# First attention of a two-layer kernel: the sums of a step's weights are taken behind the next step's scores

## The chip, the cores and the metric

The kernel runs on one core of one Trainium2 chip. A core has a matrix engine (TensorE, PE in the profile, with PEld for its loads of weights), a vector engine (VectorE, DVE), a scalar engine (ScalarE, ACT), GpSimd (POOL), and a sync engine (SyncE, SP) whose queue issues most of the transfers. Each engine works through its own queue in order, and engines wait for each other by semaphores. Matmuls write into PSUM, which this kernel cuts into two pairs of banks and four single banks; everything else lies in SBUF.

The metric is device time in microseconds. The kernel before takes 1857.02 us, the median of three runs (1854.37 to 1859.17).

## The reference

Two transformer layers follow each other on x of 4 sequences, 512 tokens, 512 channels, all in float32. Each adds an attention part and a feed-forward part to x. The change touches only the attention of the first layer:

```
def _L0_attn_ref(x, W_qkv, W_o):          # x is layer-normed before
    B, T, C = x.shape                      # 4, 512, 512
    H = 16
    D = C // H                             # 32
    qkv = jnp.einsum('btc,oc->bto', x, W_qkv).reshape(B, T, 3, H, D)
    ...
    q = _rms_norm(q * cos + _rotate_half(q) * sin)
    k = _rms_norm(k * cos + _rotate_half(k) * sin)
    scores = jnp.einsum('bhqd,bhkd->bhqk', q, k) * scale
    scores = jnp.where(causal[None, None], scores, jnp.float32(-1000000000.0))
    attn = jax.nn.softmax(scores, axis=-1)
    out = jnp.einsum('bhqk,bhkd->bhqd', attn, v)
    ...
    return jnp.einsum('btc,oc->bto', out, W_o)
```

Behind it come a gated feed-forward part with weights rounded to three values, a second layer whose attention part is a scan over time, and a second feed-forward part with an attention of its own and routed experts. They fill the span from about 424 us on.

## The kernel before

The four sequences (batches b = 0 to 3) go through the first attention one after another, from 65 to 408 us of the profile. `attend` (L345) works on one batch. Its 16 heads are taken in four groups g of four heads, and the 512 keys in four blocks j of 128. A step m is one pair (g, j), so a batch has 16 steps, and steps 4g to 4g+3 belong to group g. Because of the causal mask, key block j is met only by the queries from 128 j on: 512, 384, 256 or 128 of them.

Five small functions make up a step:

- `scores` (L355): PE multiplies queries and keys of four heads into two pairs of banks (L361). ACT takes the exponentials into the tile `pt` of that j (L366), which has one buffer. POOL then puts zeros where a query precedes its key (L367, the mask).
- `weigh` (L372): PE adds the values, weighted with `pt`, to the group's averages `av` (L377), which stay in one bank from the group's first step to its end.
- `add` (L382): for j > 0, DVE adds the weights of the block before to those of this block (L385), in place. After it, the first 128 queries of `pt` hold their sum over all key blocks, still spread over the 128 keys of a block.
- `invert` (L387): PE multiplies these 128 queries with ones, which sums over the keys (L392, into a bank `sm`), and DVE takes the reciprocals (L396). At the group's last step DVE multiplies the averages with the reciprocals into `oT` (L398), which frees the bank of `av`.

The loop from L401 to L411 lays the steps out with a lag. Within turn m of the loop:

```
scores(*steps[m])          # the new step
add(*steps[m - 2])
part()                     # what between[m] holds
weigh(*steps[m - 1])
invert(*steps[m - 2])
```

`between` (built from L458 on) holds the work of other batches that is put between the steps: projections of the next batch (`project`, eight matmuls of 128x512 at L284, 3.70 us in all, whose result DVE reads for the rotation at L296 and L300), the output projection of the batch before (`back`, L340 and L343), transposes of heads (`turn_heads`, through `transpose_into` at L132 and L133), the scaling of heads on DVE (`scale_heads`, L312 to L327), and jobs on the weights of the feed-forward part. Such a job fetches a piece of weights through SP (L218) and measures it on ACT (L234, L252) or rounds it on DVE (L201, L202); two pieces are under way at a time. Batch 3 has no projections to put in, and from its step 5 on no output projections either.

Inside this stage PE's order is that of the program text (`manual_schedule` at L417). The order on DVE, ACT and POOL is set by a planner, which simulates the kernel before it runs, keeps roughly to the program's order and pulls instructions ahead where its model has an engine free. The planner also chooses which of the four single banks a tile gets. These banks serve `av`, `sm`, the projections `pq` and `y`, and the transposes `tp`.

After the loop `attend` returns a function that ends the last step; the caller lays two transposes of heads of the next batch ahead of it (L483 to L486).

Of the kernel before, what the change touches and what calls it, by code (L numbers as in the profile page):

```python
# [46 lines left out]
def block_kernel(ctx: ExitStack, tc: tile.TileContext, a: dict, out: bass.AP):  # L47
# [16 lines left out]
    def pair(name):  # L64
        return banks["pair"].tile([P, 2, 512], F32, tag="pair", name=name)

    def bank(name):
        return banks["bank"].tile([P, 512], F32, tag="bank", name=name)
# [95 lines left out]
    with tc.tile_pool(name="a_w", bufs=1) as aw, tc.tile_pool(name="a_1", bufs=1) as a1, tc.tile_pool(  # L164
# [180 lines left out]
        def attend(b, between):  # L345

            qkT, v = turned_qk[b], values[b]
            oT = outs[b] = a1.tile([P, NK, T], F32, tag="oT", name="oT")
            weights, averages, inverses = {}, {}, {}

            def scores(g, j):  # L355
                w = T - j * P
                pt = weights[g, j] = a2.tile([P, HG, w], F32, tag=f"pt{j}", name=f"pt{j}", bufs=1)
                both = [pair("sc") for _ in range(2)]
                for i in range(HG):
                    rows = slice(i * D, (i + 1) * D)  # L360
                    nc.tensor.matmul(  # L361
                        both[i // 2][:, i % 2, :w], qkT[rows, NG + g, j * P : (j + 1) * P],
                        qkT[rows, g, j * P :], start=True, stop=True,
                    )
                for i, sc in enumerate(both):
                    nc.scalar.activation(pt[:, 2 * i : 2 * i + 2, :w], sc[:, :, :w], AF.Exp, scale=SCALE)  # L366
                nc.gpsimd.affine_select(  # L367
                    out=pt[:, :, 0:P], in_=pt[:, :, 0:P], compare_op=ALU.is_ge, fill=0.0,
                    base=0, pattern=[[0, HG], [1, P]], channel_multiplier=-1,
                )  # L370

            def weigh(g, j):  # L372
                if j == 0:
                    averages[g] = bank("av")
                for i in range(HG):
                    h = g * HG + i
                    nc.tensor.matmul(  # L377
                        averages[g][i * D : (i + 1) * D, j * P :], v[:, j, h * D : (h + 1) * D],
                        weights[g, j][:, i, :], start=j == 0, stop=j == NT - 1,
                    )  # L380

            def add(g, j):  # L382
                if j > 0:
                    pt = weights[g, j]
                    nc.vector.tensor_tensor(pt, pt, weights[g, j - 1][:, :, P:], ALU.add)  # L385

            def invert(g, j):  # L387
                if j == 0:
                    inverses[g] = a2.tile([P, T], F32, tag="r", name="r", bufs=1)
                sm = bank("sm")  # L390
                for i in range(HG):
                    nc.tensor.matmul(  # L392
                        sm[i * D : (i + 1) * D, :P], ones[:, :D], weights[g, j][:, i, :P],
                        start=True, stop=True,
                    )
                nc.vector.reciprocal(inverses[g][:, j * P : (j + 1) * P], sm[:, :P])  # L396
                if j == NT - 1:
                    nc.vector.tensor_tensor(oT[:, g, :], averages.pop(g), inverses.pop(g), ALU.mult)  # L398

            steps = [(g, j) for g in range(NG) for j in range(NT)]  # L400
            for m in range(len(steps) + 1):  # L401
                if m < len(steps):
                    scores(*steps[m])
                if m > 1:
                    add(*steps[m - 2])
                for part in between.get(m, ()):
                    part()
                if m > 0:
                    weigh(*steps[m - 1])
                if m > 1:  # L410
                    invert(*steps[m - 2])  # L411
            return lambda: (add(*steps[-1]), invert(*steps[-1]))

        def do(f, *args):
            return lambda: f(*args)
# [1 line left out]
        with tc.manual_schedule(engines={mybir.EngineType.PE}):  # L417
# [39 lines left out]
            for b in range(B):  # L457
# [20 lines left out]
                if b == B - 1:  # L478
                    first_mv = const.tile([P, NT, 2], F32, tag="mv", name="mv")
                    for t in range(NT):  # L480
                        between[9].append(do(statistics, a1, xs[0], t, first_mv))
                finish = attend(b, between)
                if b + 1 < B:  # L483
                    turn_heads(b + 1, 2)
# [302 lines left out]
    with tc.tile_pool(name="b_s", bufs=1) as bs, tc.tile_pool(name="b_1", bufs=1) as b1, tc.tile_pool(  # L787
# [79 lines left out]
        with tc.manual_schedule(engines={mybir.EngineType.PE}):  # L867
# [4 lines left out]
            for b in range(B):  # L872
# [10 lines left out]
                def part(n):  # L883
                    if n % 3 == 2 and n > 3 * 4 and b + 1 < B:
                        next(coming, None)
                        if not light[0]:
                            return
                    if n not in (2, 3, 5):
                        light[0] = next(between, False)
# [194 lines left out]
    with tc.tile_pool(name="c_1", bufs=1, reuse_waits="tile") as c1, tc.tile_pool(  # L1084
# [7 lines left out]
        steps = [(b, n, half) for b in range(B) for n in range(NS) for half in range(2)]  # L1092
# [730 lines left out]
```

## Time and profile before

| what | value |
|---|---|
| time, median of three runs | 1857.02 us |
| the profiled execution | 1858.7 us, with a span of 1857.0 us |
| mean granted TensorE clock | 0.98 |
| first attention | 65 to 408 us |
| sums, L392 on PE | 512 matmuls, median 273 ns, eight to a step |
| reciprocals, L396 on DVE | 64, median 950 ns |
| additions, L385 on DVE | 48, from 622 to 2205 ns, for 512, 1024 or 1536 elements |
| exponentials, L366 on ACT | 128, from 363 to 1026 ns, two to a step |
| mask, L367 on POOL | 64, median 635 ns, at most 2165 ns |
| product into oT, L398 on DVE | 16, median 691 ns |

A row of the timeline has the start in us, the length in us, the engine, the line, the operation, output and inputs with their shapes, and the number of instructions merged into it; in brackets stands how long the engine had been idle and what ended that. Neighbouring matmuls overlap a little at their ends, so from start to start they take somewhat less than their rows say. A row of the waits has the waiting engine, line and tile, what it waited for, and then the total in us, the number of times and the longest. A wait before a load of weights (PEld) is counted apart from PE's own.

### The profile page before, as it was taken

The numbers are of one execution on the slowest core, as the hardware profiler recorded it, in microseconds if no ns is written. First come the engines' busy times: TensorE is split into PE (matmuls) and PEld (weight loads), VectorE is DVE, ScalarE is ACT, GpSimd is POOL, SyncE is SP. The second block draws the span as 40 slices with busy tenths as digits, with TensorE's granted clock in tenths as the row PEclk, the third lists the DMA queues.
The fourth block names the chain that finished last, engine by engine and source line by source line (L and its number), as shares of the span: only waits on it lengthen the run. The fifth ranks groups of instructions, "written<-read, shape, count | busy, mean of one in ns | idle before, by whom it ended". The sixth has DMA issues, their size and how long they took to land.

```text
span 1857.0 us, 27575 instructions
## 1 busy us (share of the span) xinstructions
PE 1740.2 (94%) x10374; PEld 1093.0 (59%) x10374; DVE 1186.6 (64%) x1908; ACT 938.0 (51%) x1940; POOL 581.5 (31%) x383
## 2 busy tenths in 40 slices
PE   7899899989999998989997989999999999999998
PEld 3443344437777676878886875556556554544444
DVE  6577757786655556899887886574766764322222
ACT  2433533332242536889988867576676652111111
POOL 2231313120202021889887860100000000244431
PEclk9999999999999999999999988999999999999999
DMA  7002300102011112333223200000010006455545
GB/s 244 22 1 68 109 1 1 46 1 76 5 40 53 59 56 82 94 92 102 58 73 102 58 28 1 1 24 1 1 35 24 24 24 230 150 91 91 91 79 142
DMA packets 74630, 115.07 MB, mean 62 GB/s; under 512 B 9546, under 2 KB 34762, under 8 KB 73940
## 3 DMA queue, kind: packets, MB, share of 16 engines
q1 hardware_dynamic: 64996, 90.87, 15.4%
q0 software_dynamic: 8656, 20.32, 6.1%
q10 hardware_dynamic: 848, 2.13, 0.3%
q8 instruction: 83, 1.36, 0.3%
q14 instruction: 47, 0.39, 0.1%
HBM read 83.02 MB, written 33.42 MB: 63 GB/s over the span
## 4 chain that ended last, share of the span: by engine, by line
PE 68%; DVE 13%; ACT 11%; issue 3%; DMA 3%; POOL 1%; DVEq 0%; SPq 0%; ACTq 0%; POOLq 0%
PE pgr L1702 7%; PE pg L844 6%; PE pq L284 5%; PE ys L1153 4%; PE yr L1723 4%; PE scd L1387 4%; PE bu L1121 3%; PE y L1327 3%; PE y L862 3%; PE pge L1288 3%; PE tp L132 3%; PE bu L1116 3%; PE y L340 3%; PE tpd L1410 2%; ACT pr L1398 2%
## 5 line engine op out<-in xcount | busy, mean ns | idle before, releaser
L1140 POOL TENSOR_TENSOR hc<-h,cb 128x1024 f32<-128x1024 f32 x128 | 301.1, 2378 | 115.4 <-DVE h L1129 93.7
L1129 DVE TENSOR_TENSOR_SCAN h<-da,bu 128x512 f32<-128x512 f32 x256 | 295.1, 1204 | 28.5 <-PE bu L1121 14.3
L284 PE MATMUL pq<-wqkv,hT 128*128 128x512 f32 x384 | 179.6, 615 | 4.8 <-DVE qk L300 3.6
L1109 ACT ACTIVATE da<-delta_l,am 128x511 f32<-128x511 f32 x256 | 163.4, 709 | 2.1 <-DVE h L1129 2.0
L1398 ACT ACTIVATE pr<-scd,nm 128x128 f32<-128x128 f32 (+3 forms) x256 | 133.3, 530 | 57.6 <-DVE nm L1395 56.7
L844 PE MATMUL pg<-hTh,w 128*128 128x512 f32 (+1 forms) x352 | 145.6, 414 | 1.0 <-ACT hTh L831 0.7
L844 PE MATMUL pg<-hTl,w 128*128 128x512 f32 (+1 forms) x352 | 139.9, 397 | 0.2 <-DVE hTl L832 0.2
L1153 PE MATMUL ys<-ident,hc 128*128 128x128 f32 x1024 | 136.7, 277 | 3.3 <-DVE h L1129 1.7
L1121 PE MATMUL bu<-ident,bu 128*128 128x128 f32 x768 | 132.2, 279 | 6.4 <-ACT bu L1103 6.4
L1702 PE MATMUL pgr<-wgu,gTe 128*128 x304 | 137.1, 593 | 0.0
L1103 ACT ACTIVATE bu<-dxT,bts 128x512 f32<-128x512 f32 x192 | 124.3, 712 | 16.2 <-PE bu L1121 13.3
L284 PEld LDWEIGHTS pq<-wqkv,hT 128*128 128x128 f32 x384 | 71.5, 194 | 97.3 <-issue 91.2
L366 ACT ACTIVATE pt<-sc 128x1024 f32<-128x1024 f32 (+3 forms) x128 | 83.3, 698 | 78.0 <-PE sc L361 72.3
L1387 PE MATMUL scd<-kTd,qTd 32*128 32x512 f32 (+3 forms) x512 | 109.0, 507 | 14.0 <-ACT pr L1398 11.3
L1153 PEld LDWEIGHTS ys<-ident,hc 128*128 128x128 f32 x1024 | 119.0, 143 | 4.3 <-DVE h L1129 1.9
L1116 PE MATMUL bu<-diag_l,dxT 128*128 128x128 f32 x512 | 105.9, 289 | 16.3 <-DVE h L1129 13.3
L367 POOL TENSOR_SCALAR_AFFINE_SELECT pt<-pt 128x512 f32<-128x512 f32 x64 | 56.2, 879 | 179.1 <-ACT pt L366 156.5
L1395 DVE TENSOR_REDUCE nm<-scd 128x2 f32<-128x256 f32 (+3 forms) x128 | 105.0, 821 | 2.8
L1410 PE MATMUL tpd<-ident,pr 128*128 128x128 f32 x640 | 102.6, 290 | 3.5 <-ACT ptd L1417 1.1
L1116 PEld LDWEIGHTS bu<-diag_l,dxT 128*128 128x128 f32 x512 | 82.3, 196 | 40.0 <-DVE h L1129 23.2
L1121 PEld LDWEIGHTS bu<-ident,bu 128*128 128x128 f32 x768 | 95.6, 145 | 9.9 <-ACT bu L1103 9.9
L1709 DVE SCALAR_TENSOR_TENSOR hidr<-pgr,silr 128x256 f32<-128x256 f32 x38 | 16.1, 425 | 130.0 <-ACT silr L1707 130.0
(338 smaller groups left out, 3290.7 us busy)
## 6 DMA issues: line engine op xcount, KB each, us to landing
cb<-c_rows SPq DMA_DIRECT2D x64, 256.0 KB, 3.3
q_w<-in_w2T SPq DMA_DIRECT2D x20, 256.0 KB, 2.8
diag_l<-diags SPq DMA_DIRECT2D x64, 64.0 KB, 2.0
hrows<-h SPq DMA_DIRECT2D x4, 1024.0 KB, 4.3
acc<-x SPq DMA_DIRECT2D x16, 256.0 KB, 2.0
wgu<-in_r_gate SPq DMA_DIRECT2D x7, 512.0 KB, 9.5
wgu<-in_r_up SPq DMA_DIRECT2D x7, 512.0 KB, 10.0
wdn<-in_r_down SPq DMA_DIRECT2D x7, 512.0 KB, 9.3
```

The source lines that it names most:

```text
L284: nc.tensor.matmul(y, inputs_T[b][:, k, t * P : (t + 1) * P], wqkv[:, k, s * C : (s + 1) * C], start=k == 0, stop=k == NK - 1,)
L844: nc.tensor.matmul(pg[:rows, i, :], w[:, k, f * P : f * P + rows], part[:, k, :], start=k + m == 0, stop=k + m == NK,)
L1109: nc.scalar.activation(da[:, k, 1:], delta[:, k, 1:], AF.Exp, scale=am[:, k, n : n + 1])
L1116: nc.tensor.matmul(bu[:, :P], loaded[b][1][:, 0, k * P : (k + 1) * P], scaled[b, n][0], start=True, stop=True,)
L1121: nc.tensor.transpose(bu[:, t * P : (t + 1) * P], scaled[b, n][t][:, k * P : (k + 1) * P], ident)
L1129: nc.vector.tensor_tensor_scan(h[:, i, :], decays[b, n][:, 2 * half + i, :], bu, 0.0, ALU.mult, ALU.add)
L1140: nc.gpsimd.tensor_tensor(hc, states.pop((b, n, half)), weighed[b, n].unsqueeze(1).to_broadcast([P, 2, T]), ALU.mult)
L1153: nc.tensor.matmul(sums[b][t][:, k * P : (k + 1) * P], hc[:, i, t * P : (t + 1) * P], ident, is_transpose=True, start=n == 0 and k == 0, s ...
L1387: nc.tensor.matmul(sc[:, i, :w], qT[at, g, t * P : w], kT[at, g, :w], start=True, stop=True)
L1398: nc.scalar.activation(pr[:, i, :w], sc[:, i, :w], AF.Exp, bias=nm[:, i : i + 1], accum_out=sums[b, g][:, t, 2 * p + i : 2 * p + i + 1],)
L1410: nc.tensor.transpose(tp[:, j * P : (j + 1) * P], pr[:, i, j * P : (j + 1) * P], ident)
L1702: nc.tensor.matmul(pg, gT[:, k, :], wgu[:, bass.ds(e, 1), k, :].rearrange("p e o -> p (e o)"), start=k == 0, stop=k == NK - 1,)
```

## The change

In turn m of the loop the sums of step m - 3 are now taken right after the new step's scores and the addition, ahead of the other batches' work, where before those of step m - 2 ended the turn. Turn m = 16, which has no scores, takes the sums of step 13. After the loop the last addition and the sums of step 14 are laid down at once, and the function that is returned only takes the sums of step 15.

```diff
                     scores(*steps[m])
                 if m > 1:
                     add(*steps[m - 2])
+                if m > 2:
+                    invert(*steps[m - 3])
                 for part in between.get(m, ()):
                     part()
                 if m > 0:
                     weigh(*steps[m - 1])
-                if m > 1:
-                    invert(*steps[m - 2])
-            return lambda: (add(*steps[-1]), invert(*steps[-1]))
+            add(*steps[-1])
+            invert(*steps[-2])
+            return lambda: invert(*steps[-1])
```

On PE the order of two turns reads, before and after (w, s and p for the averages, the sums and the other batches' work):

```
before:  scores m | p | w m-1 | s m-2 | scores m+1 | p | w m | s m-1
after:   scores m | s m-3 | p | w m-1 | scores m+1 | s m-2 | p | w m
```

## The prediction

> **What bounds the kernel now.** The page's head comes first, for the whole span.
>
> ```profile
> span 1857.0 us, 27575 instructions
> PE 1740.2 (94%) x10374; PEld 1093.0 (59%) x10374; DVE 1186.6 (64%) x1908; ACT 938.0 (51%) x1940; POOL 581.5 (31%) x383
> PE 68%; DVE 13%; ACT 11%; issue 3%; DMA 3%; POOL 1%; DVEq 0%; SPq 0%; ACTq 0%; POOLq 0%
> ```
>
> The second line is busy time, the third the chain that ended last. TensorE (PE) bounds the kernel, so a change pays where PE stands still. The change touches only the first attention. Its windows, one for each batch, were cut at the batches' first scores; the columns are the stretch, its length, then PE, PEld, DVE, ACT and POOL busy, and the granted clock.
>
> ```profile
> 65.00:151.50 86.50, 80.04 (x531) 34.65 (x529) 63.80 (x104) 34.66 (x57) 25.00 (x25) 0.98 0.00 1
> 151.50:258.70 107.20, 97.11 (x565) 41.86 (x563) 79.92 (x131) 47.16 (x92) 25.82 (x25) 0.97 0.26 77
> 258.70:350.90 92.20, 89.37 (x548) 38.23 (x546) 59.96 (x96) 32.11 (x53) 24.15 (x24) 1.00 0.00 1
> 350.90:407.20 56.30, 47.31 (x425) 19.19 (x418) 45.59 (x55) 21.34 (x33) 14.49 (x16) 0.96 0.13 38
> ```
>
> PE idles 6.5, 10.1, 2.8 and 9.0 us in them, 28.4 us in all: nothing above that can come from this stage. What ended PE's idle time is in the waits, from 65 to 408 us:
>
> ```profile
> PE sm L392 <- DVE pt L385: 13.2, 15, 1.9
> PE sc L361 <- ACT pt L366: 4.2, 4, 1.8
> PE pq L284 <- DVE qk L300: 3.6, 1, 3.6
> PE av L377 <- POOL pt L367: 3.3, 2, 1.7
> ```
>
> The first row is what the change aims at: the sums (`invert`, L392) wait 15 times for VectorE's addition (`add`, L385). The likely gain is therefore a part of 13.2 us, and I go through the 15 places.
>
> **The change, part by part.** No instruction is added or removed and no DMA moves. In each batch the sums of steps 0 to 12 now stand behind the next step's scores instead of in front of them; those of 13, 14 and 15 keep their place on PE, since no scores follow there. So 52 of the 64 groups of sums trade places with one group of scores. On PE the cover that a wait gains is exactly those scores: 1.07, 0.86, 0.65 or 0.44 us from start to start for 512, 384, 256 or 128 queries (1.14, 0.93, 0.71 and 0.50 us in the rows, ends overlapping). A group of sums itself takes 0.35. On DVE the reciprocal (L396, 0.95 us) and every fourth step the product into `oT` (L398, 0.69) now come behind the next step's addition in program order. POOL and SP get nothing new. The last addition is issued ahead of two heads' transposes; the sums that need it there (148.16 us) wait for nothing now, so this is worth 0.
>
> *Ends of batches 0, 1 and 2.* Six of the 15 waits are the sums of steps 13 and 14, 0.90 and 0.62 us each time (144.17, 145.44; 251.21, 252.47; 346.61, 347.88): 4.6 us. Their order on PE is the same afterwards: gain 0.
>
> *Start of batch 0.* Before the sums of step 2 at 81.40 PE waits 0.90 us; then come scores and, at 83.01, a projection. In the new order scores 4 start at 77.85 (before 79.00), because two groups of sums come behind them and not ahead. Scores 5 then wait for the exponentials of step 4 (1.94 us for the two, L366, ending at 80.9) and end at 81.5; the sums follow, and the projection starts at 81.85. Gain 83.01 - 81.85 = 1.15 us. What follows to 150 us is PE-bound, with no DMA, so it is kept.
>
> *Steps 9 of batches 0 and 2* (109.35, 311.57; 0.55 us each). The scores cover the wait, but the projection behind stood until 110.61 because VectorE only finished reading the previous projection at 110.45 (L300, 109.78 + 0.67). That stays. Gain 0.16 each, 0.3 together.
>
> *Step 3 of batch 1.* Here the longest wait stands, and what comes after it decides:
>
> ```profile
> 173.95 0.42 PE L392 MATMUL sm<-pt,ones 128*32 128x128 f32 x8 [1.94 <-DVE pt L385]
> ...
> 188.27 0.70 PE L361 MATMUL sc<-qkT 32*128 32x256 f32 x4 [1.41 <-ACT pt L366]
> 192.58 6.09 PE L284 MATMUL pq<-wqkv,hT 128*128 128x512 f32 x8 [3.61 <-DVE qk L300]
> ```
>
> The scores would fill 1.07 of 1.94 us. But at 192.58 PE waits for VectorE, which stands behind a weight piece on its way from memory (L201 at 190.59 after 2.33 us for a DMA); the chain from 173.8 to there is DMA, L201, L202, DMA again, with no matmul in it. What is gained at 174 is waited for again at 188 and 192. I take 0; the other end is 1.07.
>
> *Batch 3, from 376 us on.* Here no projections lie between the steps, and PE, ACT, POOL and DVE wait for one another in turn. In this timeline is the third group of heads:
>
> ```profile
> 388.84 0.96 DVE L396 RECIPROCAL r<-sm 128x128 f32<-128x128 f32 x1 [1.32 <-PE sm L392]
> ...
> 389.83 0.69 DVE L398 TENSOR_TENSOR oT<-av,r 128x512 f32<-128x512 f32 x1
> ...
> 390.45 1.76 DVE L385 TENSOR_TENSOR pt<-pt,pt 128x1536 f32<-128x1536 f32 x1
> ...
> 390.60 2.69 POOL L367 TENSOR_SCALAR_AFFINE_SELECT pt<-pt 128x512 f32<-128x512 f32 x2 [1.19 <-ACT pt L366]
> ...
> 392.76 0.64 PE L377 MATMUL av<-pt,v 128*32 128x256 f32 x8 [1.68 <-POOL pt L367]
> ```
>
> A mask (L367) that takes 0.63 us alone stretches to about 2.1 beside an addition, and PE waits 1.68 us for it. A group of four steps takes 10.07 us (the reciprocals at 388.84 and 398.91). VectorE's own work in it is 1.68 + 1.90 for the additions, 4 x 0.87 and 0.61, from start to start: 7.7 us. PE's is 7.4. So at most 2.4 us a group are there. I ran the new order by hand with these durations. Weights 6 (the averages' matmuls, L377) start at 381.25 (before 381.51). The sums of step 5 come behind scores 8, the 0.97 us at 383.12 are covered, and weights 8 start at 385.95 (387.49). In the next group, scores 10 stand ahead of the sums of step 7; VectorE then does reciprocal and product (1.55 us) before it starts the long addition at 389.5, when the mask of step 10 has run from 388.7 to 389.35. The collision above goes; what is late next is that addition itself, which the sums of step 9 meet at 391.2. Weights 12 start at 394.1 (397.56): 8.15 us a group. At the end, the addition of step 14 is issued ahead of the reciprocal of 13, and the chain of VectorE's last additions, reciprocals and product closes at 405.6 (409.05). The last sums end at 403.45, where the output projection starts (407.23). Gain 3.8 us; the ends are 1.9 (the DVE waits at 383.12, 385.88 and 395.77 shortened, the collision kept) and 5.1 (all VectorE idle there: 4.6 us before reciprocals, 0.5 before additions).
>
> **Rules weighed.** Row first: the addition that starts 0.15 us ahead of a mask keeps its 1.76 us and the mask waits; at 380.82 a mask starts 0.04 us ahead, keeps 0.64, and the addition takes 2.21. The Trainium skill, "SBUF — State Buffer", section "SBUF: two separate sides", says that the first to start holds the pair of ports and the other blocks. That speaks against part of my chain: a mask that now comes first holds up the addition, on the engine that nearly bounds the tail. By the rule's full 0.63 us in three groups the tail loses 1.9 us and gains 1.9; by the row of 380.86 (2.21 - 1.76 = 0.45) it loses 1.35. In my chain the mask ends 0.15 us before the addition starts, so I take neither, and 1.9 is the low end named above.
>
> Second: in the window 404.00:407.20 the clock is 0.76, and 0.50 from 407.2 to 412.5, after gaps of 1.94 and 0.16 us. "TensorE: Matmul & The Clock Gate", Part 1, asks for an idle window of about 3.4 us before the clock halves; by it, gaps this short should cost nothing. The row decides: the half clock costs 5.3 / 2 = 2.65 us. The new tail has gaps of 1.3 and 1.25 us at the same place, so I leave the cost in; by the rule the sum would be 2.65 larger.
>
> **Sum.** 0 + 1.15 + 0.3 + 0 + 3.8 = 5.3 us (1.15 and 0.3 belong to batches 0 and 2). Later stages start earlier by it; they are PE-bound. Against the profiled execution, 1858.7 us with a span of 1857.0, that is 1853.4. The median shown, 1857.02, lies 1.7 below that execution, so the forecast is **1851.7 us**. Its own range, from 1.9 in the tail without the small gains to 5.1 with 1.07 of batch 1, is a gain of 2 to 7.6 us: 1849 to 1855.
>
> **Rivals.** *More.* VectorE's and ACT's order is the planner's, and the moved sums give it new ready times. If it puts the reading of the projection ahead of L201 at 190.59, the 3.61 us at 192.58 go, or the half clock at 407 does (2.65). For it: one position in a queue decides. Against: nothing in the change touches that position. Gain 5.3 + 3.6, 1848 us.
>
> *Nothing in the tail.* The planner lets the reciprocals keep their place ahead of the additions; then the collision at 390.5 stays, scores no longer help, and only 1.15 + 0.3 remain: 1855.5 us. The change then does on PE what it says and not on VectorE. For it: at 171.33 and 107.71 a reciprocal already runs ahead of a ready addition.
>
> *Slower: banks.* Two averages are open from the weights of a new group to the product of the old one, and there are four banks. Now the sums come right in front of the projection of steps 6, 10 and 14, with no scores between. If that projection gets the bank which the product frees, PE waits for reciprocal and product after the sums, 0.95 + 0.61 and about 0.2 of handing over, 1.75 us, at three places in three batches: 15.8 us. Net 15.8 - 5.3 = 10.5 slower, 1867.5 us. It turns the sign from four such places on. For it: 110.61 is a wait of this kind, and the slack at 88.50 is 0.4 us (previous read done at 88.10). Against: the bank of the previous projection comes free first, and the time from it to the next one is unchanged, since sums and scores only trade places.
>
> **Numbers.** Forecast 0.58, more 0.12, nothing in the tail 0.08, slower 0.22. A difference of 0.3%, 5.6 us, is about what a measurement of this kernel can tell from no change. The forecast lies on that line, so half of its 0.58 counts as faster, half as same: faster 0.29 + 0.12 = 0.41, same 0.29 + 0.08 = 0.37, slower 0.22. The range from 1846 to 1864 leaves out some 0.04 below, and above it the part of the bank case with more than seven places, 0.14.
>
> **What would show it.** Right: the sums' wait falls from 13.2 us to 6 to 8, of which 4.6 at the ends of batches 0 to 2; the third group in the tail takes 8 to 8.5 us; no mask of 2.1 us ends a wait of the averages; the wait at 192.58 grows by about 1 us. Wrong: a new row of projections (L284) or averages waiting for L396 or L398, which is the bank case; or a tail group still of 10 us.

## The result: slower by 0.23%

The changed kernel takes 1862.52 us (median of 14 runs, 1858.21 to 1866.45), the kernel before 1856.95 us (14 runs, 1854.01 to 1860.89): a ratio of 1.0023, 95% interval 1.0013 to 1.0033 (the quotient of the two medians, 1.0030, lies at the upper end). The prediction had 1851.7. The profiled execution took 1860.61 us. From the changed kernel's page, its span and busy times:

```profile
span 1858.9 us, 27568 instructions
PE 1750.1 (94%) x10374; PEld 1093.1 (59%) x10374; DVE 1180.3 (63%) x1908; ACT 938.3 (50%) x1940; POOL 586.4 (32%) x383
```

The second line holds the first clue: the same 10374 matmuls keep PE busy 9.9 us longer than before (1740.2). POOL, too, is busy 4.9 us longer with the same 383 instructions. Work that was only moved has become longer. The batches' windows, cut again at the first scores (the columns are those of the prediction):

```profile
63.40:151.20 87.80, 81.22 (x529) 33.56 (x528) 61.68 (x104) 34.53 (x57) 27.09 (x25) 1.00 0.00 1
151.20:262.50 111.30, 102.46 (x563) 42.82 (x562) 77.30 (x131) 47.36 (x92) 27.02 (x25) 0.94 0.25 74
262.50:358.20 95.70, 92.02 (x547) 37.29 (x546) 59.23 (x96) 32.19 (x53) 25.75 (x24) 1.00 0.00 1
358.20:411.70 53.50, 48.28 (x422) 18.74 (x418) 45.21 (x55) 21.48 (x33) 14.26 (x16) 0.95 0.15 41
```

By the exact starts of the scores, batch 3 has become 2.8 us shorter and the others 1.3, 4.2 and 3.6 longer, 6.3 us in all. In batch 2 PE's busy time makes 2.65 us of it (92.02 after 89.37), and POOL is busy 1.6 us longer (25.75 after 24.15); the clock is 1.00 and the DMA share 0.00 as before. Below are PE's waits from 63 to 412 us.

```profile
PE sm L392 <- DVE pt L385: 8.8, 9, 1.8
PE sc L361 <- ACT pt L366: 7.1, 11, 1.8
PE pq L284 <- DVE qk L300: 4.9, 3, 3.2
```

The sums wait 4.4 us less and the averages no longer wait for a mask, as was meant; scores and projections wait 4.2 us more. These rows explain no loss. To find it I cut the stage into turns, from the first scores of one step to those of the next (the last turn of a batch ends at the next batch's scores, that of batch 3 at the output projection). Changed kernel minus before, first profiles, us:

| turns | batch 0 | batch 1 | batch 2 | batch 3 |
|---|---|---|---|---|
| first ones (0 to 5; 0 to 6; 0 to 2; 0 to 2) | -1.88 | +0.13 | -0.22 | -0.23 |
| the others, which nothing disturbs | +0.73 | +0.58 | +1.20 | +0.29 |
| 8 to 10 | +1.82 | +1.72 | +1.91 | |
| 15, the end of a batch | +0.66 | +1.80 | +0.66 | |
| 5 to 15 of batch 3 | | | | -2.87 |

So there are three losses that the prediction priced at nothing: in the undisturbed turns, in turns 8 to 10, and at the ends of batches.

**Theory P: the place on PE.** Here are the same two turns of batch 2 on PE, before and then after:

```profile
273.24 0.85 PE L377 MATMUL av<-pt,v 128*32 128x384 f32 x8
273.90 0.40 PE L392 MATMUL sm<-pt,ones 128*32 128x128 f32 x8
274.24 0.50 PE L361 MATMUL sc<-qkT 32*128 32x128 f32 x8
274.67 3.70 PE L340 MATMUL y<-wo,oT 128*128 128x512 f32 x8
278.30 0.64 PE L377 MATMUL av<-pt,v 128*32 128x256 f32 x8
```

```profile
276.96 0.85 PE L377 MATMUL av<-pt,v 128*32 128x384 f32 x8
277.75 0.50 PE L361 MATMUL sc<-qkT 32*128 32x128 f32 x8
278.18 0.43 PE L392 MATMUL sm<-pt,ones 128*32 128x128 f32 x8
278.54 3.70 PE L340 MATMUL y<-wo,oT 128*128 128x512 f32 x8
282.17 0.64 PE L377 MATMUL av<-pt,v 128*32 128x256 f32 x8
```

Nothing waits in either, and the durations are the same within 0.03 us. But from the first averages to the next it is 5.06 us before and 5.21 after. Start to start, averages to sums take 0.66, but averages to scores 0.79; sums to scores take 0.34, sums to the projection 0.36. So rows with the same form of matmul (128*32 for averages and sums, 32*128 for scores, 128*128 for projections: the shape behind the input names) overlap more at their seam than rows of different form. It is the form that counts, and not that another piece of work begins: in the kernel before, projections are followed by transposes, both 128*128.

```profile
121.13 3.70 PE L284 MATMUL pq<-wqkv,hT 128*128 128x512 f32 x8
124.67 1.04 PE L132 MATMUL tp<-ident,qk 128*128 128x128 f32 x8
```

From start to start these take 3.54 us, a projection and averages of another form 3.63 (274.67 to 278.30 above). The ends of matmuls are modelled in a profile, so starts are compared. Turns of 4.85, 5.28 and 5.70 us became 4.99, 5.41 and 5.84.

**Theory V: VectorE's order.** In turns 8 to 10 there is more. First before, then after, in batch 2:

```profile
300.86 0.95 DVE L396 RECIPROCAL r<-sm 128x128 f32<-128x128 f32 x1
301.02 1.27 POOL L303 TENSOR_TENSOR qk<-qk,rot 128x512 f32<-128x512 f32 x1 [1.69 <-DVE qk L300]
301.72 1.65 DVE L385 TENSOR_TENSOR pt<-pt,pt 128x1024 f32<-128x1024 f32 x1
```

```profile
306.30 1.21 DVE L385 TENSOR_TENSOR pt<-pt,pt 128x1024 f32<-128x1024 f32 x1
306.47 2.17 POOL L303 TENSOR_TENSOR qk<-qk,rot 128x512 f32<-128x512 f32 x1 [2.94 <-DVE qk L300]
308.67 0.63 ACT L305 ACTIVATE sqk<-qk 128x512 f32<-128x512 f32 x1 [5.07 <-POOL qk L303]
309.21 1.92 ACT L366 ACTIVATE pt<-sc 128x1024 f32<-128x1024 f32 x2
...
310.27 1.83 PE L361 MATMUL sc<-qkT 32*128 32x384 f32 x8 [0.39 <-ACT pt L366]
```

Before, a reciprocal separates the reading of a projection (L300) from the addition, and POOL's rotation (L303) runs beside the reciprocal in 1.27 us. The rotation has started first there, and the addition is the one that is held: 1.65 us, where it takes 1.21 in the other order. After, the reciprocal comes earlier, the addition follows the reading at once and starts 0.17 us ahead of the rotation, and now the rotation is held: 2.17 us (2.70 a turn earlier, beside a longer addition). Everything behind it is late: the squares (L305), the exponentials that queue behind the squares on ACT, the next scores, which now take 1.83 us instead of 0.93 because their second pair of banks comes free late (its loads of weights start at 311.18, those of the first at 310.26), and the scaling of heads. What speaks for this chain is that the longest rotation was 1.65 us before and is 2.71 now.

**The ends of batches.** Six waits of 0.90 and 0.62 us were to stay. VectorE and PE at the end of batch 0, before and after:

```profile
142.34 3.04 DVE L385 TENSOR_TENSOR pt<-pt,pt 128x1536 f32<-128x1536 f32 x2
144.17 0.43 PE L392 MATMUL sm<-pt,ones 128*32 128x128 f32 x8 [0.90 <-DVE pt L385]
145.44 0.42 PE L392 MATMUL sm<-pt,ones 128*32 128x128 f32 x8 [0.62 <-DVE pt L385]
```

```profile
142.78 0.94 DVE L396 RECIPROCAL r<-sm 128x128 f32<-128x128 f32 x1
143.01 0.43 PE L392 MATMUL sm<-pt,ones 128*32 128x128 f32 x8 [0.54 <-DVE pt L385]
143.65 1.15 DVE L385 TENSOR_TENSOR pt<-pt,pt 128x1024 f32<-128x1024 f32 x1
144.86 0.42 PE L392 MATMUL sm<-pt,ones 128*32 128x128 f32 x8 [1.21 <-DVE pt L385]
```

Before, both additions ran back to back (x2 in 3.04). After, the reciprocal of step 12 comes between them: 0.54 + 1.21 instead of 0.90 + 0.62. And turn 15 holds one group of sums more, which turn 2 has lost. Together +0.66; in batch 1 a spell of half clock (0.50 from 256.0 to 259.2) adds 1.14, in both profiles of the changed kernel. Why it falls there is not shown.

### The profile page after: what moved, and what is told of

Read it like the earlier page. It is cut to its first block, busy times and chain, and to the rows that moved or that the text cites. A ratio compares the mean times of both kernels' runs of the same rounds, so it can differ in the third digit from the quotient of the medians.

```text
span 1858.9 us, 27568 instructions
## 1 busy us (share of the span) xinstructions
PE 1750.1 (94%) x10374; PEld 1093.1 (59%) x10374; DVE 1180.3 (63%) x1908; ACT 938.3 (50%) x1940; POOL 586.4 (32%) x383
## 4 chain that ended last, share of the span: by engine, by line
PE 69%; DVE 13%; ACT 10%; issue 3%; DMA 3%; POOL 2%; SPq 0%; DVEq 0%; ACTq 0%; POOLq 0%
PE pgr L1704 7%; PE pg L846 7%; PE pq L284 5%; PE ys L1155 4%; PE scd L1389 4%; PE yr L1725 4%; PE bu L1123 3%; PE y L1329 3%; PE y L864 3%; PE pge L1290 3%; PE bu L1118 3%; PE tp L132 3%; PE tpd L1412 3%; PE y L340 2%; ACT pr L1400 2%
## 5 line engine op out<-in xcount | busy, mean ns | idle before, releaser
L367 POOL TENSOR_SCALAR_AFFINE_SELECT pt<-pt 128x512 f32<-128x512 f32 x64 | 50.3, 786 | 168.9 <-ACT pt L366 145.8
## 6 DMA issues: line engine op xcount, KB each, us to landing
cb<-c_rows SPq DMA_DIRECT2D x64, 256.0 KB, 3.2
q_w<-in_w2T SPq DMA_DIRECT2D x20, 256.0 KB, 2.7
acc<-x SPq DMA_DIRECT2D x16, 256.0 KB, 2.0
```

## The experiments

All timed runs are compared with the kernel before on the same chip. Rival to P and V is the bank case of the prediction (B). The cuts of code leave lines out at `...`.

**1. New order in batch 3 alone.**

```diff
+                late = b == B - 1
+                if late and m > 2:
+                    invert(*steps[m - 3])
...
-                if m > 1:
+                if not late and m > 1:
                     invert(*steps[m - 2])
+            if late:
+                add(*steps[-1])
+                invert(*steps[-2])
+                return lambda: invert(*steps[-1])
```

> The new order is kept in batch 3 only; batches 0 to 2 have the old one. All theories: batches 0 to 2 take 86.5, 107.0 and 92.2 us from first scores to first scores as before, batch 3 takes 53.5 as after, total about 2.8 us below before (1854). If batch 3 alone does not keep its 2.8 us, the tail's gain belongs to something that the earlier batches hand over.

Measured: 1850.1 us (6 runs), ratio 0.9954 (0.9938 to 0.9970). Batch 3 takes 53.51 us, as in the changed kernel; the turns of batches 0 to 2 are back to 4.85, 5.28, 5.70. So the tail gains, and what is lost lies in batches 0 to 2. The stage is 2.9 us shorter than before, the time 7.5: see experiment 6.

**2. Only VectorE's order.** The sums stay in their old place on PE, and reciprocal and product come one turn later, behind the next addition:

```diff
-                sm = bank("sm")
+                sm = sums[g, j] = bank("sm")
...
+            def finish_step(g, j):
+                sm = sums.pop((g, j))
                 nc.vector.reciprocal(inverses[g][:, j * P : (j + 1) * P], sm[:, :P])
...
                 if m > 1:
                     add(*steps[m - 2])
+                if m > 2:
+                    finish_step(*steps[m - 3])
```

> TensorE keeps the order of before; only the reciprocals and products are issued one turn later, so VectorE has after's order, in which an addition follows directly on the reading of a projection. Theory P (what costs is the place of the sums on TensorE, where they no longer run into the averages): turns with a projection take 4.85 and 5.28 us as before, total within 2 us of before. Theory V (what costs is VectorE's order, which makes the addition hold up POOL's rotation): POOL's rotations take 2.2 to 2.7 us in the turns 7, 8 and 11 as after, turns 8 to 10 are 1 to 1.5 us longer in each of batches 0 to 2, total 3 to 5 us above before. Theory B (banks): as before, the averages are freed a little later, total within 1 us.

Measured: 1861.23 us (18 runs), ratio 1.0022 (1.0013 to 1.0032). Undisturbed turns are 4.85 and 5.28, the old values. Turns 8 to 10 take 18.94, 18.85 and 19.06 us, against 17.23, 17.79 and 17.36: 4.5 us in all. In the timeline of batch 0 is the same picture as after the change:

```profile
100.10 1.22 DVE L385 TENSOR_TENSOR pt<-pt,pt 128x1024 f32<-128x1024 f32 x1
100.27 2.17 POOL L303 TENSOR_TENSOR qk<-qk,rot 128x512 f32<-128x512 f32 x1 [2.95 <-DVE qk L300]
...
104.07 1.83 PE L361 MATMUL sc<-qkT 32*128 32x384 f32 x8 [0.46 <-ACT pt L366]
```

VectorE's order alone costs as much as the whole change, which has gains in it too, with PE's order untouched. It is shown as a cause of its own. The edit also holds the bank of the sums a turn longer; PE waits 1.6 us in all for the reciprocals that free it (L399).

**3 and 4. One step later, but beside the averages.** The sums of step m - 3 stand in front of the averages of turn m (3) or behind them (4), so neighbours have one form again. Both in one cut, with marks that are not in the code; the end of the loop is that of the changed kernel:

```diff
                 for part in between.get(m, ()):
                     part()
+                if m > 2:
+                    invert(*steps[m - 3])     # 3
                 if m > 0:
                     weigh(*steps[m - 1])
+                if m > 2:
+                    invert(*steps[m - 3])     # 4
```

> The sums of step m-3 stand right in front of the averages of step m-1, behind the other batches' work. P: averages and sums are neighbours again, turns take 4.85 to 4.90 and 5.28 to 5.33 us instead of 4.99 and 5.41, the tail keeps its gain; total 3 to 6 us below before. V: VectorE has before's order (reading, reciprocal, addition) and the rotations take 1.27 us again; about the same sum. B: the averages' bank is held longer than after, so projections of turns 6, 10 and 14 wait 1 us or more; total above after.

> The sums of step m-3 stand behind the averages of step m-1, where before those of step m-2 stood: a whole step later and with before's neighbours. P: turns of 4.85 and 5.28 us exactly, exponentials covered by the sums as before; V: VectorE's order is before's; both: waits of the sums for the addition nearly gone, 3 to 6 us below before. B: as in the run beside, with the averages held longest: waits of projections at turns 7, 11 and 15, total above after.

Measured: 1858.28 us, ratio 1.0005 (0.9996 to 1.0013), and 1857.5, ratio 1.0002 (0.9991 to 1.0013), 14 runs each. Turns 3 and 4 of batch 2 are 4.85 and 5.28 in both, though the sums are as late as in the changed kernel. The seam in experiment 4:

```profile
277.18 0.64 PE L377 MATMUL av<-pt,v 128*32 128x256 f32 x8
277.64 0.40 PE L392 MATMUL sm<-pt,ones 128*32 128x128 f32 x8
277.97 1.14 PE L361 MATMUL sc<-qkT 32*128 32x512 f32 x8
```

Averages to sums 0.46, sums to scores 0.33, as before. The longest rotations are 1.50 and 1.64 us, so V is gone too. Both runs win the lost time back, and neither wins the 3 to 6 us that were expected: in 4 the sums wait only 2.4 us instead of 13.2, but projections then wait 5.5 us for VectorE's readings instead of 3.6, turn 7 is 5.06, and the stage is 341.7 us against 342.0. In 3 it is even 345.3: turn 7 is 5.07, turns 12 and 13 take 6.47 and 7.26 instead of 6.25 and 6.99, and the ends of batches 0 and 1 14.91 and 14.78 instead of 13.16. In these forms, covering the waits in batches 0 to 2 brought nothing.

**5. PE's new order with VectorE's old one,** held by an order of issue: reading (`latest["read"]`, L300 of the kernel before), reciprocal, addition.

```diff
+                    with tc.issue_after(latest.get("recip", latest["read"]).ins):
                         nc.vector.tensor_tensor(pt, pt, weights[g, j - 1][:, :, P:], ALU.add)
...
+                with tc.issue_after(latest["read"].ins):
+                    latest["recip"] = nc.vector.reciprocal(inverses[g][:, j * P : (j + 1) * P], sm[:, :P])
...
+                if m > 2:
+                    invert(*steps[m - 3])
                 if m > 1:
                     add(*steps[m - 2])
-                if m > 2:
-                    invert(*steps[m - 3])
```

> TensorE's order is that of the changed kernel; VectorE's is held to that of the kernel before: reading of a projection, reciprocal, addition. Theory P (the place of the sums on TensorE costs about 0.14 us in each of some 36 turns that hold work of another batch): these turns stay at 4.99, 5.41 and 5.84 us. Theory V (the addition that follows the reading directly meets GpSimd's rotation): the longest rotation falls from 2.7 to under 1.6 us, and turns 8 to 10 of batches 0 to 2, together 19.1 to 19.5 us in the changed kernel, fall to about 17.8 (17.3 of before and three times 0.14). Both theories: about 1858.5 us, ratio 1.001. P alone true and V not: the turns 8 to 10 stay, 1862. V alone the cause of the whole loss: 4.85 and 5.28 return, and about 1853.

Measured: 1876.85 us (6 runs), ratio 1.0096 (1.0080 to 1.0112), a miss. The rotations are at most 1.50 us and the undisturbed turns 4.99, 5.41 and 5.84: P stands without V's collision. Turn 8 is back at 5.41 in all three batches, which is P alone, after 5.88, 6.14 and 5.88: there the collision had cost 0.5 to 0.7 us. But turns 8 to 10 together stay at 18.8, 18.3 and 19.0. The first row is a wait of VectorE in this run, the second the same wait in the changed kernel:

```profile
DVE r L399 <- PE sm L394: 32.1, 27, 2.9
DVE r L396 <- PE sm L392: 7.6, 8, 2.2
```

With the sums behind the scores, a reciprocal that must go first makes VectorE stand, and the additions, readings and sums behind it are late. The old order on VectorE belongs to the old place on PE. Beyond turn 8, how much of V is the collision alone and how much the shifted order is therefore not separated.

**6. The first run once more, with its own profile.**

> The new order in batch 3 alone once more, with its own profile. Its stage was 2.9 us shorter than before, its time 7.5 us. If the other 4.6 were the granted clock and the spread between executions, the stage comes out at 339 to 340 us again, and the time between 1852 and 1856 (ratio about 0.998). If the changed order does something behind the stage, the ratio is 0.995 again, and the feed-forward part, 296.0 against 297.8 us in the first profile, is as short again.

Measured: 1849.77 us (6 runs), ratio 0.9952 (0.9939 to 0.9965). The stage is 338.6 us, 3.4 shorter than in the first profile of before and 1.2 than in the second (experiment 10). The gain in time is real and again larger than the stage. Two parts of the rest can be named. The mean granted clock over the runs was 0.9795 against 0.9777 for before; within the runs of before 0.001 goes with 0.7 to 1.2 us, so some 1.8 us by estimate. And behind the stage, at 649 us, PE waits in the kernel before for a cast on ACT (L855), since ACT stands in a copy that waits for an earlier transfer. Before, two rows; then this run:

```profile
648.09 0.59 ACT L659 COPY st<-tpd 128x512 f32<-128x512 f32 x1 [2.05 <-DMA dxs<-st]
...
649.25 0.50 PE L862 MATMUL y<-w,gh 85*128 85x512 f32 x1 [1.65 <-ACT gh L855]
```

```profile
642.37 0.59 ACT L666 COPY st<-tpd 128x512 f32<-128x512 f32 x1 [0.52 <-DMA dxs<-st]
```

Such waits for the cast add up to 1.4 to 2.2 us in both profiles of before, both of the changed kernel and in experiments 2, 3, 4, 9 and 12, and at most 0.4 in 1, 5, 6, 7 and 8. Why the transfer lands sooner there stays open. Behind the stage the second profile of before took 1449.6 us, as the first (1449.7), and 1, 6, 7 and 8 took 1444.2 to 1447.5, which speaks for a gain there; but experiment 2 has 1445.6, without the new order on PE, so single profiles do not settle it.

**7 and 8. Two more forms of the same.** In 7 the sums of batch 3 stand in front of the averages, behind the other work. In 8 they stand so too, and steps 0 to 5 of batch 0 have the new place as well:

```diff
+            early = 6 if b == 0 else 0
...
+                if 2 < m < early:
+                    invert(*steps[m - 3])
```

> New order in batch 3 alone, and there the sums directly ahead of the averages, behind what is done of batch 2. Theory P: turns 2, 3 and 4 of batch 3 are 5.06, 4.99, 5.41 us with the sums behind the scores; beside the averages they are 5.28 or less, 4.85 and 5.28, so batch 3 is about 0.3 us shorter than 53.5 and the time 0.3 below the run with the new order in batch 3 alone. If the place is worth nothing: the same 53.5.

> As the last, and the sums one step later in steps 0 to 5 of batch 0 too, where no other batch's work lies between: the old order from step 6 on. The changed kernel had batch 0 at its sixth step 1.9 us ahead of before, the run with the new order in batch 3 alone 0.5 behind. Theory: 1.5 to 2 us of it are kept, since from step 6 on VectorE's and TensorE's order are those of before: batch 0 about 85 us, the time about 1.5 below the run with the new order in batch 3 alone. Rival: the lead is lost by step 9, where TensorE waits for other work in both; then no difference.

Measured: 1847.92 us (5 runs), ratio 0.9955 (0.9941 to 0.9968), and 1851.36 (5 runs), ratio 0.9965 (0.9952 to 0.9978). Turns 3 and 4 of batch 3 came out as P has it: 4.85 and 5.28 in both. Batch 3 is 53.25 us in 8, 0.3 shorter as expected, and 51.54 in 7, where a spell of half clock in turn 1 (8.08 us in experiments 1, 6 and 8, 6.38 here) did not fall. In time 1, 6, 7 and 8 can't be told apart; all four beat both kernels. The head brought nothing, against the 1.5 to 2 us expected: turns 2 to 5 of batch 0 took 15.75 us (15.84 in experiment 6), and turn 6 grew by 1.0.

**9. The new place in turns 13 to 15 of batches 0 to 2 alone.**

```diff
+                moved = m > 11 and b < B - 1
...
+                if moved and m > 12:
+                    invert(*steps[m - 3])
...
-                if m > 1:
+                if m > 1 and not moved:
```

> The order of before, but in batches 0 to 2 the sums stand between scores and projection from step 13 on, one step later. Theory P: turn 12 loses a group of sums (6.25 to about 5.9 us), turns 13 and 14 are 7.13 and 5.41 us instead of 6.98 and 5.27, and the end of a batch, where a reciprocal now comes between two additions and one more group of sums stands, grows by 0.6 us; together about 0.6 per batch, the time 1.5 to 2 us above before (ratio 1.001). If the place is worth nothing and only VectorE's order in steps 7 to 10 made the loss: 6.99, 5.27, and no difference from before.

Measured: 1861.29 us (22 runs), ratio 1.0020 (1.0010 to 1.0031). Turns 12 to 15 are 5.93, 7.12, 5.41 and 13.81, in all three batches alike (10.60 for the last in batch 2, 9.94 before): 0.6 a batch, as expected, with longest rotations of 1.64. The other half of the 3.7 us is not found: the profiled execution, 1857.56 us, is the third fastest of the 22 and no slower than before, though a spell of half clock falls at 390 us in it, in batch 3, whose order was not touched. The mean granted clock over the runs was 0.9763 against 0.9777, by the estimate of experiment 6 some 1.4 us.

**10 and 11. Both kernels once more, for a second profile each.**

> The kernel before once more, for a second profile. Its first profile had 342.0 us in the attention stage and 1449.8 behind it, where the runs with the new order in batch 3 alone had 1445.4 and 1447.5. If the stretch behind the stage merely varies between executions, this one comes out anywhere between 1444 and 1451; the stage itself again 342 within 1.5 us. If the new order in batch 3 really shortens what follows, this one has 1449 to 1451 again.

> The changed kernel once more, for a second profile. The turns that hold work of another batch again 4.99, 5.41 and 5.84 us, the rotations of steps 7 and 8 again 2.7 and 2.2 us, the stage 348 within 1.5 us, if all this is the kernel's and not that one execution's.

Measured, one run each: 1854.41 and 1864.59 us. Batch 2 is 92.17 before and 95.73 after, to 0.01 us as in the first profiles, turns of 4.99 and 5.41 and rotations of 2.71 and 2.17 included. The stages are 339.7 and 351.6 us, so the 1.5 us of both expectations were too narrow, and the two pairs of stages differ by 6.3 and by 11.8 us. One place of the spread can be shown: PE's row from 72 to 78 us, in batch 0, in the first and the second profile of the changed kernel (length, busy times, then the granted clock):

```profile
72.00:78.00 6.00, 5.22 (x64) 2.06 (x64) 4.27 (x5) 3.81 (x7) 2.67 (x3) 1.00 0.01 3
72.00:78.00 6.00, 6.00 (x44) 2.15 (x44) 3.38 (x3) 1.58 (x4) 2.07 (x3) 0.50 0.01 3
```

One program, the same gap of 1.75 us in front: once no half clock, once six microseconds of it. Turns 2 to 5 take 14.15 us in the first and 17.10 in the second; before they take 16.03 and 15.82, with 3.4 us of half clock in both.

**12. The dose: one more change of form.** The sums in the middle of a projection (`project`, and in the same way `back`), against the changed kernel:

```diff
             for k in range(NK):
+                if k == NK // 2 and midway:
+                    midway.pop()()
...
                 if m > 2:
-                    invert(*steps[m - 3])
+                    midway.append(lambda: invert(*steps[m - 3]))
```

> As the changed kernel, but the sums of a step stand in the middle of the other batches' projection: four of its matmuls, the sums, the other four. Theory M (each change between the forms 128*32, 32*128 and 128*128 costs TensorE about 0.14 us): a turn has 3 changes before, 4 in the changed kernel and 5 here, so turns of 4.85, 4.99 us become 5.13, and 5.27, 5.41 become 5.55. Rival N (the sums only lose their overlap with the averages, once): 4.99 and 5.41 as in the changed kernel. By M some 36 turns lose 0.14 us more, and where VectorE's order stays, the time is about 1867; by N it stays near 1862.5.

Measured: 1866.43 us (8 runs), ratio 1.0055 (1.0034 to 1.0075). PE in batch 2:

```profile
282.21 1.98 PE L346 MATMUL y<-wo,oT 128*128 128x512 f32 x4
284.12 0.43 PE L398 MATMUL sm<-pt,ones 128*32 128x128 f32 x8
284.48 1.98 PE L346 MATMUL y<-wo,oT 128*128 128x512 f32 x4
286.39 0.64 PE L383 MATMUL av<-pt,v 128*32 128x256 f32 x8
```

The two halves take 1.91 us each from start to start, 3.82 against 3.63 in one piece. Turns are 5.19 and 5.61: with 3, 4 and 5 changes of form a turn takes 4.85, 4.99 and 5.19, or 5.28, 5.41 and 5.61. The rival, one lost overlap with the averages, is refuted. The time was expected at about 1867 us, but not all of it is the forms: turn 9 of batches 0 and 2 takes 8.77 us instead of 6.74, since the sums wait 1.76 us for a reciprocal there. The Trainium skill states a rule that fits, in "TensorEngine Tiling (Array Packing)", section "Key Properties": "Changing tiling mode (not just tile) drains the TensorE". It gives no figure; here one change costs 0.14 to 0.20 us. That the cost is a drain no run here shows by itself.

## Why the prediction was wrong

**The step that failed** is the sentence "52 of the 64 groups of sums trade places with one group of scores", with a price of nothing for the trade and, in the bank rival, "the time from it to the next one is unchanged, since sums and scores only trade places". The cover that a wait gains was counted; the seams were not. Before, the sums are glued to averages of their own form; behind the scores they stand between two other forms. At 0.14 us a turn this makes some 4 us: 2.8 in the undisturbed turns of the table and 1.3 in turns 8 to 10, if these lose the same. No wait shows it. It is in the starts of neighbouring rows of before, where a batch's first averages have no sums behind them:

```profile
70.82 1.07 PE L377 MATMUL av<-pt,v 128*32 128x512 f32 x8
71.82 0.70 PE L361 MATMUL sc<-qkT 32*128 32x256 f32 x4
...
86.64 1.07 PE L377 MATMUL av<-pt,v 128*32 128x512 f32 x8
87.52 0.40 PE L392 MATMUL sm<-pt,ones 128*32 128x128 f32 x8
```

The same averages take 1.00 us to scores and 0.88 to sums. What the prediction named as signs did not help: the tail group of 8 to 8.5 us and the end of the long mask appeared, the sums' wait came close (8.8 us), and no sign of being wrong did. All of them are waits or lie in the tail.

**VectorE's order** was used only where it helps, in the tail. In batches 0 to 2 the same shift takes the reciprocal from between the reading and the addition, and the addition starts ahead of the rotation instead of behind it: turns 8 to 10 lose 4.2 us beyond P. The rule that the prediction weighed for masks ("SBUF — State Buffer", "SBUF: two separate sides": the first to start holds the pair of ports, the other blocks) holds here to 0.2 us: the addition ends at 306.30 + 1.21 = 307.51, and a rotation of 1.27 us that ends at 308.64 would have started at 307.37. I weighed it for one pair of instructions and not for every neighbour of VectorE's additions on POOL.

**The ends of batches,** priced at 0 because PE's order there is unchanged, cost 0.66 each: VectorE's order is not unchanged, and a group of sums moved in.

**Start of batch 0,** 1.15 us predicted: the first profile shows 1.88, the second a loss of 1.1 to 1.3, and experiment 8 nothing. Its argument, "PE-bound, with no DMA, so it is kept", left the clock out: before has 3.4 us of half clock there in both profiles, the changed kernel none in the first and 6.8 us in the second. The size is not settled.

**Step 9 of batches 0 and 2,** 0.3: drowned in V. **Step 3 of batch 1,** 0: turns 0 to 6 differ by 0.13 in the first profiles, though the wait at 192 did not grow by 1 us (3.19 after 3.61). But there the changed kernel has a spell of half clock at 181 us that before has not. Its second profile has only the spell at 191 that the first of before has too, and between these two the turns are 0.9 us shorter after. So the agreement is luck, and the other end, 1.07, was nearer.

**The tail** was right in mechanism and too large in size: 2.9 us from step 5 on, the same within 0.1 in every run with the new order in front of the averages there and VectorE's order left to the planner (1, 3, 6, 7, 8, 11, 12), against 3.8. A group takes 8.38 us (scores at 391.61 and 399.99) where 8.15 was worked out; the mask of 2.1 us has gone from PE's waits. At the end the planner put two reciprocals in front of the last addition, not behind it:

```profile
408.76 1.75 DVE L396 RECIPROCAL r<-sm 128x128 f32<-128x128 f32 x2
410.44 0.62 DVE L385 TENSOR_TENSOR pt<-pt,pt 128x512 f32<-128x512 f32 x1
411.12 0.66 PE L392 MATMUL sm<-pt,ones 128*32 128x128 f32 x8 [1.80 <-DVE pt L385]
```

**The bank rival** had the sign but not the cause: no projection or average waits for the product (L398) in the changed kernel. Added up, 4.1 (P) + 4.2 (V) + 3.1 (ends) - 2.9 (tail) - 1.9 (start of batch 0, that execution) - 0.3 (one group of sums less and the rest) is the 6.3 us of the first pair of profiles. The medians differ by 5.6; that the two agree proves little, since the second pair differs by 11.8.

## What to carry to other kernels

Where PE is the bound, moving a small group of matmuls is not free even if nothing waits: count the changes between forms (row-tiled, column-tiled, full) before and after, and read the price from seams that the trace already has. A shift on one engine must be followed on the engines whose order a planner sets: list every pair that shares a port or a queue and see which pairs become neighbours. And ask where a wait is worth covering: here the 2.9 us of the tail were there for a change in one batch, while the larger sum of waits elsewhere, even when it fell from 13.2 to 2.4 us, brought nothing in experiment 4.

## What the runs showed of the hardware beside that

Scores whose two pairs of banks come free one after the other take 1.83 us instead of 0.93 at a granted clock of 1.00 (310.27 in the changed kernel): the two pairs of row-tiled matmuls no longer run side by side. And a gap on PE of 1.75 us was followed by half clock in one execution and not in the other of one program; in this stage every spell of half clock in the traces lasts 3.41 us or a whole multiple of it, up to 13.65. Such spells, of 1 to 3 us each in cost, make most of the difference between two profiles of one kernel here.
